# Two points per VectorE operation, and units of scores folded across eight steps

## The chip, the cores and the metric

The kernel runs on one core of one Trainium2 chip, everything in float32. The metric is device time in microseconds, the median of repeated executions of the whole program. PE is TensorE, DVE VectorE, ACT ScalarE, POOL GpSimd, SP SyncE.

## The reference, cut to what matters

Four layers run one after another on x of shape (2, 512, 32, 32). The change lies in the first, a deformable attention with 8 groups of 64 channels, whose keys are 64 sampled points per group. For each of 2 x 8 groups, 1024 pixels (queries) and 64 points (keys) a small network gives a bias from the pixel's position relative to the point:

```python
pos  = grid_q[:, :, None, :] - grid_kv[:, None, :, :]          # (16, 1024, 64, 2)
bias = sign(pos) * log1p(abs(pos))
bias = relu(bias @ cpb_w1 + cpb_b1)                            # 2 -> 128   first layer
bias = relu(bias @ cpb_w2 + cpb_b2)                            # 128 -> 128 second layer
bias = (bias @ cpb_w3 + cpb_b3).reshape(b, GROUPS, H*W, Hd*Wd) # 128 -> 1   third layer
sim  = einsum('bhid,bhjd->bhij', qh, kh) + bias
attn = softmax(sim, axis=-1)
out  = einsum('bhij,bhjd->bhid', attn, vh)
```

Then follow a projection, an MLP, and three more attention layers, which the change leaves alone.

## The kernel before

**Tiles, steps, points.** Layer 0 works through NT = 8 tiles of scores. A tile holds two groups: 128 points on the partitions and 1024 pixels along them. It is made in 32 steps of four points, so the main loop has 256 steps; t is the tile of a step i, i // 32.

**First layer (`first`, L599).** The sign-log of the position splits into a part in x and a part in y, each a table of 32 numbers per point. The tables of a tile are written to DRAM (`slog_d`, L471), read back for 16 points at a time, broadcast over the partitions (`load_tabs`, L573), and scaled by `cpb_w1`. One DVE operation per point adds the x row and the y row for 32 x 32 pixels and clamps at zero; its result, 128 hidden units by 1024 pixels, goes to one of the 11 places of `ring`. It is issued 7 points ahead of its use (AHEAD).

**Second layer (`second`, L616, L625).** The 128 hidden units of the second layer are sorted by the sign of `cpb_w3` into four parts of 32. For each part PE multiplies four points side by side (128x32 weights, each point in its own 32 columns of the array) for two halves of 512 pixels into `z`; ACT adds the bias and takes the relu. The four points of a step are on partitions 32 point to 32 point + 31.

**Joins and folds.** DVE joins parts 0 and 1 and parts 2 and 3 with the turned sign (`joined`, L630). The rest of the sum over hidden units is done by DMA: the second join is added to the first (L934, issued from GpSimd), then the partitions of a unit are folded in half (L927), and in half again, now into the shared unit of four steps: for the unit's first step in place (L929), for the three others by a copy on SP (L931) of one half and an add on GpSimd (L937) of the other. `joins[i]` is the unit of step i; its room comes from six places of `bridge` for units that others are folded into, and from a ring of four (`h2j`) for the others.

**Third layer (`third`, L645).** Four shared units (16 steps) at a time are multiplied by weights of plus and minus ones (`w3_16`), which sum what is left over partitions and put each point in its row of `sim`. That is done twice per tile, at steps 20 and 36 counted from the tile's first. Then `scores` (L653) adds query times key, and `finish` does the softmax in the steps behind (ACT copy, PE transposes, DVE maximum, ACT exponentials).

The order in each engine is that of the program (`in_order`): each of the four parts of a step (k = 0 to 3) issues its own pieces. The generator `behind` puts the softmax of the last tile (`finish`), the offsets of the tile after next (`offsets`, with DVE reductions at L414) and the samples of the next (`samples`) into the same order, one piece after every second part. The last 16 steps use units of two steps, and the loop ends in `finish_last`.

A buffer comes free when its last reader is done; the framework's waits are semaphores between engines and on DMAs. GpSimd's and SP's queues are in order too: a DMA whose wait isn't met holds those behind it.

Of the kernel before, what the change touches and what calls it, by code (L numbers as in the profile page):

```python
# [12 lines left out]
F32 = mybir.dt.float32  # L13
# [6 lines left out]
P = 128  # L20
# [59 lines left out]
def kernel(ctx: ExitStack, tc: tile.TileContext, a: dict, out: bass.AP):  # L80
# [111 lines left out]
    def layer0(l0, fold_d, t2_b, o2_b):  # L192
# [6 lines left out]
        h2q = l0.enter_context(tc.tile_pool(name="att_h2q", bufs=3))  # L199
        h2p = cycle([bridge[:, k, :] for k in range(6)])  # L200
        h2j = cycle([bridge[:, 6, :], bridge[:, 7, :], *(one.tile([P, HW], F32, name=f"h2j{k}") for k in range(2))])
# [18 lines left out]
        qkw = next(h2j).rearrange("p (j q n) -> p j q n", j=2, q=NPAIR)  # L220
# [15 lines left out]
        ring = [one.tile([P, HW], F32, name=f"h1{k}") for k in range(3)]  # L236
        ring += [qkv2.rearrange("p k n -> p (k n)")[:, k * HW : (k + 1) * HW] for k in range(6)]
        ring += [proj2.rearrange("p k n -> p (k n)")[:, k * HW : (k + 1) * HW] for k in range(2)]
# [13 lines left out]
        ones = one.tile([P, P], F32, name="ones")  # L252
        nc.gpsimd.memset(ones, 1.0)
# [25 lines left out]
        w3_16 = one.tile([P, 48], F32, name="w3_16")  # L279
# [7 lines left out]
        def bias_weights():  # L287
            sort = h2b.tile([P, 7, P], F32, name="sort", tag="h2")
            row, below, w2t = [sort[:, k, :] for k in range(3)]
            perm = sort[:, 3:, :].rearrange("p b (r u) -> p b r u", u=32)  # L290
            few = one.tile([P, 28], F32, name="few")
# [69 lines left out]
            quarter = few[:, 26:28]  # L361
            for k in range(2):
                nc.vector.tensor_reduce(quarter[:, k : k + 1], ident[:, 2 + k : P : 4], AX.X, ALU.add)
                nc.vector.scalar_tensor_tensor(eighth, quarter[:, k : k + 1], 8.0, eighth, ALU.mult, ALU.add)
            nc.vector.tensor_scalar(w3_16[:, 16:32], row[:, 0:16], eighth, 0.0, ALU.add, ALU.is_equal)
            nc.vector.tensor_scalar(w3_16[:, 16:32], w3_16[:, 16:32], w3sign[:, 1:2], None, ALU.mult)
# [15 lines left out]
        def offsets(t):  # L382
# [88 lines left out]
            nc.sync.dma_start(out=slog_d[t].rearrange("x p i -> p x i"), in_=pos)  # L471
# [13 lines left out]
        def samples(t):  # L485
# [25 lines left out]
            wx = one.tile([P, P], F32, name="wx")  # L511
# [17 lines left out]
            shift = one.tile([P, P], F32, name="shift")  # L529
# [12 lines left out]
            kq = one.tile([P, P], F32, name="kq")  # L542
# [3 lines left out]
            values = one.tile([P, P], F32, name="values")  # L546
# [12 lines left out]
        NCH = NR // 4  # L559
        LAST = NT * NR - 16  # L560
        tabs_of = {}

        def load_tabs(c):
# [4 lines left out]
            for ax in range(2):  # L568
                src = slog_d[t, ax].rearrange("(q r) i -> q r i", q=4)
                tab = two.tile([P, 16, 32], F32, name=f"tab{ax}")  # L570
                if 4 * c < LAST:
                    q, r = rc % 4, rc // 4 * 16
# [16 lines left out]
        def first(p):  # L589

            chunk, point = divmod(p, 16)
            if point == 0:
                tabs_of.pop(chunk - 1, None)
                if chunk + 1 < NT * NCH:
                    load_tabs(chunk + 1)
            tx, ty = tabs_of[chunk]
            h1 = ring[p % len(ring)]

            nc.vector._custom_dve(  # L599
                TENSOR_ADD_SAT,  # L600
                out=h1.rearrange("p (y x) -> p y x", x=W),
                in0=tx[:, point, :].unsqueeze(1).to_broadcast([P, H, W]),
                in1=ty[:, point, :].unsqueeze(2).to_broadcast([P, H, W]),
                s0=float(np.finfo(np.float32).max),
                s1=0.0,
            )
            return h1

        def second(i, h1s, part):
# [3 lines left out]
            for half in range(2):  # L613
                n = slice(half * HALF, (half + 1) * HALF)
                for point in range(4):
# [3 lines left out]
                        h1s[point][:, n],  # L619
# [3 lines left out]
            ring = h2q if part % 2 else h2b if part else h2j if i % (4 if i < LAST else 2) else h2p  # L623
            h2 = ring.tile([P, HW], F32, name="h2", tag="h2") if ring in (h2q, h2b) else next(ring)
# [10 lines left out]
        def third(sim, r, h2s, fours=(), halves=range(2), wide=False):  # L635

            for half in halves:
                n = slice(half * HALF, (half + 1) * HALF)
                w = w3_16[:, 16 - r : 48 - r] if wide else w3[:, 24 - r : 56 - r]
# [17 lines left out]
        def finish(t, sim):  # L657
# [4 lines left out]
            simb = one.tile([P, HW], F32, name="simb", tag="simb")  # L662
# [11 lines left out]
            at = one.tile([P, 8, P], F32, name="at", tag="simb")  # L674
# [42 lines left out]
        def finish_last(sim, eights, fours, right_sums, left_sums):  # L717
# [7 lines left out]
            simb = one.tile([P, HW], F32, name="simb", tag="simb")  # L725
# [90 lines left out]
        nat = [[next(h2p).rearrange("p (k n) -> p k n", k=2) for _ in range(2)] for _ in range(3)]  # L816
# [68 lines left out]
        h1s, parts, joins, sim, w1s = {}, {}, {}, None, None  # L885
        behind = chain(small_steps, offsets(1), samples(0))
        AHEAD = 7

        for p in range(AHEAD):
            h1s[p] = first(p)  # L890
        late_loads()
        for i in range(steps):
            for k, part in enumerate((1, 0, 3, 2)):
# [3 lines left out]
                if p < 4 * steps:  # L897
                    h1s[p] = first(p)
                due = i - 20
                if k == 1 and 0 <= due < LAST and due % 16 == 0:  # L900
                    t, r = divmod(due, NR)
                    if r == 0:
                        sim = ps_s.tile([P, HW], F32, name="sim")
                    third(sim, r, [joins.pop(due + j) for j in range(0, 16, 4)], wide=True)
                    if r:
# [10 lines left out]
                if LAST <= i - 2 and i < steps - 2:  # L916
# [4 lines left out]
                    if i - 3 >= LAST and i % 2 and k == 3:  # L921
                        nc.gpsimd.dma_start(out=joins[i - 3][1:P:2], in_=joins.pop(i - 2)[1:P:2], accum_op=ALU.add)
                if 0 <= i - 2 < LAST:
                    j = (i - 2) % 4
# [1347 lines left out]
```

## Time and profile before

| | |
|---|---|
| median of 3 runs | 3350.77 us (3349.29 to 3352.3) |
| the profiled execution | 3353.46 us, of which span 3351.7 us |
| granted PE clock, mean | 0.998 |
| main loop of layer 0 | from 59.6 us, its last step's joins at 1983.5 us |
| first layer, L599 | 1024 operations, mean 1216 ns |
| joins, L630 | 512 operations, mean 1276 to 1277 ns |
| second layer, L616 | 16384 matmuls, each about 593 ns, four at a time |
| third layer, L645 | 280 matmuls |

Times in a profile are from one execution, counted from the start of its span. L12 is line 12 of the kernel. In a line of a group or of the timeline, `out<-in` are the names of the tiles, xN is the number of instructions; "idle before" or a bracket is the time in which the engine stood still ahead of it, with what ended that. PEld is the loading of weights, which overlaps PE. A line of the table of stretches gives, for each of PE, PEld, DVE, ACT and POOL, the busy us (and the instructions), then the granted clock, the share in which the DMA engines were busy, and GB/s.

### The profile page before, as it was taken

To read this page: it belongs to the slowest core of one execution; us is meant where nothing else is said; L and a number is where in the kernel's file an instruction comes from. 1 tells how busy PE (TensorE), PEld (TensorE's weight loads), DVE (VectorE), ACT (ScalarE), POOL (GpSimd) and SP (SyncE) were. 2 spreads that over 40 slices of the span, in tenths; PEclk is the share of its full clock that TensorE was granted. 3 is DMA by queue.
4 is the path that set the end of the run, shared out by engine and by line. 5 is a ranking of instruction groups with operands and counts; after the bars stand their busy time and mean duration, and the time that the engine had idled before them with its cause. 6 is when DMAs were issued, how large, how long until landed. Compare 5 with 4: busy or idle time off the path is not lost.

```text
span 3351.7 us, 61808 instructions
## 1 busy us (share of the span) xinstructions
PE 3323.8 (99%) x24813; PEld 1611.7 (48%) x24813; DVE 2673.0 (80%) x3540; ACT 1805.5 (54%) x2774; POOL 676.7 (20%) x804
## 2 busy tenths in 40 slices
PE   9999999999999999999999999999999999999999
PEld 4333333332333332333333339999953443687777
DVE  6999999999999799999999976455446465665556
ACT  4866877877877577877877652122136245122221
POOL 0333333333333233333333310000000000000000
PEclk9999999999999999999999999999999999999999
DMA  5778787787787577787787751000100000000111
GB/s 166 157 161 166 153 168 156 152 166 153 158 167 155 103 162 155 159 169 152 158 166 157 161 135 58 14 8 14 52 0 14 26 29 20 7 7 3 30 32 36
DMA packets 142488, 343.97 MB, mean 103 GB/s; under 512 B 36464, under 2 KB 51440, under 8 KB 141424
## 3 DMA queue, kind: packets, MB, share of 16 engines
q0 software_dynamic: 68400, 231.26, 36.5%
q1 hardware_dynamic: 72496, 103.95, 10.7%
q8 instruction: 197, 3.23, 0.4%
q10 hardware_dynamic: 1296, 4.72, 0.4%
q14 instruction: 99, 0.81, 0.1%
HBM read 71.46 MB, written 10.83 MB: 25 GB/s over the span
## 4 chain that ended last, share of the span: by engine, by line
PE 82%; DVE 9%; issue 5%; DMA 2%; ACT 1%; POOL 1%; DVEq 0%; SPq 0%; POOLq 0%; ACTq 0%
PE z L616 38%; PE pma L135 6%; PE pw L1435 6%; PE pmb L135 5%; PE pmv L1435 4%; PE score L1614 3%; PE pv L1626 3%; DVE wa L599 3%; PE pm L1435 3%; PE score L1435 3%; PE pmt L1435 1%; PE ppr L1435 1%; DVE h L599 1%; DMA bridge<-h 1%; DVE bridge L630 1%
## 5 line engine op out<-in xcount | busy, mean ns | idle before, releaser
L616 PE MATMUL z<-wa,cpb_w 128*32 128x512 f32 x11904 | 1779.2, 593 | 5.8 <-ACT h L625 3.7
L625 ACT ACTIVATE h<-z,b2h 128x1024 f32<-128x1024 f32 x768 | 851.3, 1114 | 347.9 <-PE z L616 310.6
L616 PE MATMUL z<-h,cpb_w 128*32 128x512 f32 x4480 | 983.2, 593 | 1.6 <-ACT h L625 1.6
L616 PEld LDWEIGHTS z<-wa,cpb_w 128*32 128x32 f32 x11904 | 497.2, 110 | 888.2 <-issue 778.1
L599 DVE CUSTOM_DVE_ANT_1 wa<-tab,tab 128x1024 f32<-128x1024 f32 x744 | 878.1, 1216 | 1.3 <-PE z L616 1.1
L616 PEld LDWEIGHTS z<-h,cpb_w 128*32 128x32 f32 x4480 | 256.6, 110 | 328.6 <-issue 292.1
L599 DVE CUSTOM_DVE_ANT_1 h<-tab,tab 128x1024 f32<-128x1024 f32 x280 | 332.9, 1216 | 2.3 <-PE z L616 2.2
L630 DVE SCALAR_TENSOR_TENSOR h<-h,turn,h 128x1024 f32<-128x1024 f32 x256 | 326.8, 1276 | 4.3 <-ACT h L625 4.3
L625 ACT ACTIVATE bridge<-z,b2h 128x1024 f32<-128x1024 f32 x162 | 180.8, 1116 | 121.4 <-PE z L616 119.0
L927 POOL DMA_DIRECT2D bridge<-bridge x150 | 127.6, 850 | 547.2 <-DMA bridge<-h 510.5
L630 DVE SCALAR_TENSOR_TENSOR bridge<-bridge,turn,h 128x1024 f32<-128x1024 f32 x162 | 206.8, 1277 | 4.2 <-ACT bridge L625 4.2
L934 POOL DMA_DIRECT2D bridge<-h x161 | 163.4, 1015 | 213.2 <-DVE h L630 123.6
L1278 ACT COPY p<-pma 128x128 f32<-128x128 f32 x80 | 21.3, 266 | 334.7 <-PE pma L135 334.7
L1270 DVE TENSOR_TENSOR upper<-pma,p 128x256 f32<-128x256 f32 x80 | 33.7, 422 | 178.6 <-ACT p L1278 178.5
L1615 ACT ACTIVATE p<-score 128x512 f32<-128x512 f32 x256 | 130.0, 624 | 81.2 <-PE score L1614 79.6
L927 POOL DMA_DIRECT2D h2j<-h2j x90 | 76.2, 847 | 323.0 <-DMA h2j<-h 293.6
L1647 DVE TENSOR_TENSOR acc<-acc,p 128x1024 f32<-128x1024 f32 x96 | 111.0, 1217 | 19.4 <-ACT p L1615 19.3
L625 ACT ACTIVATE h2j<-z,b2h 128x1024 f32<-128x1024 f32 x94 | 105.0, 1117 | 37.9 <-PE z L616 37.3
L1614 PE MATMUL score<-q,k 64*128 64x512 f32 x512 | 120.7, 604 | 1.1 <-DVE gm L1191 1.1
L630 DVE SCALAR_TENSOR_TENSOR h2j<-h2j,turn,h 128x1024 f32<-128x1024 f32 x94 | 120.0, 1276 | 0.0
L1626 PE MATMUL pv<-p,vT 128*64 128x512 f32 x512 | 116.5, 598 | 0.0
L937 POOL DMA_DIRECT2D bridge<-h2j x90 | 111.9, 1244 | 2.6 <-issue 1.8
(458 smaller groups left out, 4379.8 us busy)
## 6 DMA issues: line engine op xcount, KB each, us to landing
bridge<-h POOLq DMA_DIRECT2D x161, 512.0 KB, 5.5
h2j<-h POOLq DMA_DIRECT2D x94, 512.0 KB, 5.9
bridge<-bridge POOLq DMA_DIRECT2D x159, 256.0 KB, 3.9
tab<-slog_d SPq DMA_DIRECT2D x128, 256.0 KB, 4.6
h2j<-h2j POOLq DMA_DIRECT2D x90, 256.0 KB, 3.2
bridge<-bridge POOLq DMA_DIRECT2D x150, 128.0 KB, 5.4
bridge<-bridge SPq DMA_DIRECT2D x90, 128.0 KB, 3.7
bridge<-h2j SPq DMA_DIRECT2D x90, 128.0 KB, 3.6
```

The costliest lines, as they stand in the source:

```text
L135: nc.tensor.matmul(pm, w, m, start=(k == 0), stop=(k == len(pairs) - 1))
L599: nc.vector._custom_dve(TENSOR_ADD_SAT, out=h1.rearrange("p (y x) -> p y x", x=W), in0=tx[:, point, :].unsqueeze(1).to_broadcast([P, H, W] ...
L616: nc.tensor.matmul(z[point * 32 : point * 32 + 32, n], cpb_w2[:, lo : lo + 32], h1s[point][:, n], start=True, stop=True,)
L625: nc.scalar.activation(h2, z, AF.Relu, bias=b2h[:, part : part + 1])
L630: nc.vector.scalar_tensor_tensor(h2, h2, turn[:, part // 2 : part // 2 + 1], parts.pop(part + 1), ALU.mult, ALU.add)
L927: nc.gpsimd.dma_start(out=own[0:P:2], in_=own[1:P:2], accum_op=ALU.add)
L934: nc.gpsimd.dma_start(out=joins[i - 1], in_=other, accum_op=ALU.add)
L937: nc.gpsimd.dma_start(out=joins[i - 3 - j][j:P:4], in_=joins.pop(i - 3)[2:P:4], accum_op=ALU.add)
L1435: nc.tensor.matmul(out, stationary(l, k), moving(r, k), start=start and k == 0, stop=k == nk - 1, skip_group_check=not start,)
L1614: nc.tensor.matmul(sc, ks[m][r, s * P : (s + 1) * P], qs[m][r, n], start=True, stop=True)
L1615: nc.scalar.activation(p[:, part], sc, AF.Exp, scale=64 ** -0.5)
L1626: nc.tensor.matmul(pv[half][part * 64 : part * 64 + 64], vt[s % 4][:, lo : lo + 64], lps[s, half][:, part, :], start=(s == 0), stop=(s == 7),)
```

## The change

1. One DVE operation of `first` makes two points. The y table is stored in DRAM with the two points of a pair interleaved, by two DMAs of single numbers beside the one for x. The results of a pair lie interleaved by rows of 32 pixels, so `second` reads each point as 16 runs of 32. `ring` has 6 places of two points, AHEAD is 8.
2. For the first seven tiles a shared unit holds eight steps instead of four: every unit is folded in half twice and then a third time into the shared unit, one step later. The third layer then runs once per tile, at step 37 counted from its first, with the weights `w3_32`. In the last tile the units are as before.
3. Room for units comes from one queue of ten places (`room`), to which a place returns when its unit has been folded away or read by the third layer. ACT's results of parts 1 and 3 get four places in place of three (`h2q`). A few small tiles share places to make room.
4. `bias_weights` makes the further weights, with more small DVE operations; its `ones` is set by DVE.

```diff
-        h2q = l0.enter_context(tc.tile_pool(name="att_h2q", bufs=3))
-        h2p = cycle([bridge[:, k, :] for k in range(6)])
-        h2j = cycle([bridge[:, 6, :], bridge[:, 7, :], *(one.tile([P, HW], F32, name=f"h2j{k}") for k in range(2))])
+        h2q = l0.enter_context(tc.tile_pool(name="att_h2q", bufs=4))
+        room = deque([bridge[:, 7, :], *(one.tile([P, HW], F32, name=f"h2j{k}") for k in range(2))])
+        room += [bridge[:, k, :] for k in range(7)]
...
-        ring = [one.tile([P, HW], F32, name=f"h1{k}") for k in range(3)]
-        ring += [qkv2.rearrange("p k n -> p (k n)")[:, k * HW : (k + 1) * HW] for k in range(6)]
-        ring += [proj2.rearrange("p k n -> p (k n)")[:, k * HW : (k + 1) * HW] for k in range(2)]
+        ring = [one.tile([P, 2 * HW], F32, name=f"h1{k}") for k in range(2)]
+        ring += [qkv2.rearrange("p k n -> p (k n)")[:, k * 2 * HW : (k + 1) * 2 * HW] for k in range(3)]
+        ring.append(proj2.rearrange("p k n -> p (k n)"))
...
+            digit = few[:, 26:29]
+            for k, (lo, step) in enumerate(((2, 4), (3, 4), (4, 8))):
+                nc.vector.tensor_reduce(digit[:, k : k + 1], ident[:, lo:P:step], AX.X, ALU.add)
...
+            for lo in range(5, 8):
+                nc.vector.tensor_reduce(odd, ident[:, lo:P:8], AX.X, ALU.add)
+                nc.vector.tensor_add(digit[:, 2:3], digit[:, 2:3], odd)
+            nc.vector.scalar_tensor_tensor(eighth, digit[:, 2:3], 16.0, eighth, ALU.mult, ALU.add)
+            nc.vector.tensor_scalar(w3_32, row[:, 0:32], eighth, 0.0, ALU.add, ALU.is_equal)
...
-            nc.sync.dma_start(out=slog_d[t].rearrange("x p i -> p x i"), in_=pos)
+            nc.sync.dma_start(out=slog_d[t, 0], in_=pos[:, 0, :])
+            pairs = slog_d[t, 1].rearrange("(a k) i -> a (k i)", k=2).rearrange("a (i k) -> k a i", k=2)
+            with nc.allow_non_contiguous_dma("4096 numbers"):
+                for k in range(2):
+                    nc.sync.dma_start(out=pairs[k], in_=pos[k:P:2, 1, :])
...
+        WIDE = (NT - 1) * NR
         LAST = NT * NR - 16
+
+        def shared(i):
+            return 8 if i < WIDE else 4 if i < LAST else 2
...
-            tx, ty = tabs_of[chunk]
-            h1 = ring[p % len(ring)]
+            tx, ty = [tab[:, point : point + 2, :] for tab in tabs_of[chunk]]
+            h1 = ring[p // 2 % len(ring)].rearrange("p (y k x) -> p y k x", k=2, x=W)
             nc.vector._custom_dve(
                 TENSOR_ADD_SAT,
-                out=h1.rearrange("p (y x) -> p y x", x=W),
-                in0=tx[:, point, :].unsqueeze(1).to_broadcast([P, H, W]),
-                in1=ty[:, point, :].unsqueeze(2).to_broadcast([P, H, W]),
+                out=h1,
+                in0=tx.unsqueeze(1).to_broadcast([P, H, 2, W]),
+                in1=ty.rearrange("p k y -> p (k y)")
+                .rearrange("p (y k) -> p y k", k=2)
+                .unsqueeze(3)
+                .to_broadcast([P, H, 2, W]),
...
-            return h1
+            return [h1[:, :, k, :] for k in range(2)]
...
-                        h1s[point][:, n],
+                        h1s[point][:, half * 16 : half * 16 + 16, :],
...
-        AHEAD = 7
+        AHEAD = 8
...
-                if p < 4 * steps:
-                    h1s[p] = first(p)
-                due = i - 20
-                if k == 1 and 0 <= due < LAST and due % 16 == 0:
-                    t, r = divmod(due, NR)
-                    if r == 0:
-                        sim = ps_s.tile([P, HW], F32, name="sim")
-                    third(sim, r, [joins.pop(due + j) for j in range(0, 16, 4)], wide=True)
-                    if r:
+                if p < 4 * steps and k % 2 == 0:
+                    h1s[p], h1s[p + 1] = first(p)
+                for due, n in ((i - 37, 8), (i - 20, 4)):
+                    if k != 1 or not 0 <= due < LAST or due % NR or shared(due) != n:
+                        continue
+                    t = due // NR
+                    sim = ps_s.tile([P, HW], F32, name="sim")
+                    third(sim, 0, [taken(due + j) for j in range(0, 4 * n, n)], wide=w3_32 if n == 8 else w3_16)
+                    if n == 8:
                         assert next(behind, None) is None
                         scores(t, sim)
...
-                    j = (i - 2) % 4
-                    whole, own = joins[i - 2 - j], joins[i - 2]
+                    own, n = joins[i - 2], shared(i - 2)
+                    whole, j = joins[i - 2 - (i - 2) % n], (i - 2) % n
                     if k == 0:
                         nc.gpsimd.dma_start(out=own[0:P:2], in_=own[1:P:2], accum_op=ALU.add)
-                    if k == 3 and j == 0:
+                    if k == 3 and (n == 8 or j == 0):
                         nc.gpsimd.dma_start(out=own[0:P:4], in_=own[2:P:4], accum_op=ALU.add)
-                    if k == 3 and j:
+                    elif k == 3:
                         nc.sync.dma_start(out=whole[j:P:4], in_=own[0:P:4])
+                if k == 2 and 0 <= i - 3 < WIDE:
+                    own, j = joins[i - 3], (i - 3) % 8
+                    if j:
+                        nc.sync.dma_start(out=joins[i - 3 - j][j:P:8], in_=own[0:P:8])
+                    else:
+                        nc.gpsimd.dma_start(out=own[0:P:8], in_=own[4:P:8], accum_op=ALU.add)
...
-                j = (i - 3) % 4
-                if k == 1 and 0 <= i - 3 < LAST and j:
-                    nc.gpsimd.dma_start(
-                        out=joins[i - 3 - j][j:P:4], in_=joins.pop(i - 3)[2:P:4], accum_op=ALU.add
-                    )
+                for at in (i - 4, i - 3):
+                    if k != 1 or at < 0 or at >= LAST or (shared(at) == 8) != (at == i - 4):
+                        continue
+                    n = shared(at)
+                    j = at % n
+                    if j:
+                        own = taken(at)
+                        nc.gpsimd.dma_start(
+                            out=joins[at - j][j:P:n], in_=own[n // 2 : P : n], accum_op=ALU.add
+                        )
```

`taken(i)` takes the unit of step i out of `joins` and returns its place to `room`.

## The prediction

> **What bounds the kernel now.** I read the page first, for the shares and the chain that ended last.
>
> ```profile
> span 3351.7 us, 61808 instructions
> PE 3323.8 (99%) x24813; PEld 1611.7 (48%) x24813; DVE 2673.0 (80%) x3540; ACT 1805.5 (54%) x2774; POOL 676.7 (20%) x804
> ```
>
> Everything that the change touches lies in layer 0, whose loop over 256 steps runs from 59.6 to about 1982 us. So the next views are of that loop: busy time in one stretch of 238 us (one tile of scores, 32 steps), then the chain in order of time near the loop's end.
>
> ```profile
> 300.00:538.00 238.00, 236.94 (x2152) 75.10 (x2148) 232.53 (x213) 180.55 (x251) 83.84 (x97) 1.00 0.78 159
> ```
>
> ```profile
> 1899.82 49.78 PE z L616 x464
> 1949.61 1.72 PE sim L645 x16
> 1951.32 30.90 PE z L616 x288
> ```
>
> PE is busy for 236.94 of 238 us and DVE for 232.53: two engines near their limit. The chain is PE. Its 464 records are 116 passes of four matmuls side by side, 49.78 / 116 = 0.429 us a pass; 16 passes make a step, 6.87 us. The third layer (L645) stands in that chain as 1.72 us, four passes, with nothing beside it on PE.
>
> DVE's timeline, in a stretch without other work:
>
> ```profile
> 254.25 2.35 DVE L599 CUSTOM_DVE_ANT_1 wa<-tab,tab 128x1024 f32<-128x1024 f32 x2
> 256.53 1.28 DVE L630 SCALAR_TENSOR_TENSOR bridge<-bridge,turn,h 128x1024 f32<-128x1024 f32 x1
> 257.72 2.35 DVE L599 CUSTOM_DVE_ANT_1 wa<-tab,tab 128x1024 f32<-128x1024 f32 x2
> ```
>
> Two first-layer operations take 2.28 us start to start and a join 1.19, so DVE needs 2 x 3.47 = 6.94 us a step where PE needs 6.87. DVE loses 0.07 us a step there and about 0.9 in each step with a reduction of `products` (L414, mean 971 ns). The timeline shows where this leads: a join starts 1.9 us behind the ACT result that it reads in step 43 and 7.3 to 7.5 us behind in steps 49 to 51. Then PE pauses:
>
> ```profile
> 450.62 3.62 PE L616 MATMUL z<-wa,cpb_w 128*32 128x512 f32 x32
> 454.78 1.50 PE L616 MATMUL z<-wa,cpb_w 128*32 128x512 f32 x12 [0.55 <-ACT h L625]
> ```
>
> Eight passes from 450.62 should end at 454.05; the next starts 0.73 later. Adding up all starts of passes from 59.6 to 1992 us, pauses of over 0.12 us sum to 14.7 us: 1.9 are waits of L645 for a fold (1.46 and 0.39), 0.9 lies in the last tile's finish, and 11.9 come where DVE is late (mostly 0.7 behind `po` and 0.7 some steps later, in each tile). So PE's own work is the bound, and DVE's lateness is worth at most 12 us.
>
> Third comes GpSimd's queue, which issues the accumulating DMAs in order.
>
> ```profile
> 269.40 0.83 POOL L927 DMA_DIRECT2D bridge<-bridge  x1 [4.55 <-DMA bridge<-h]
> 269.93 1.22 POOL L934 DMA_DIRECT2D bridge<-h  x1
> 270.50 1.51 POOL L937 DMA_DIRECT2D bridge<-h2j  x1
> 275.68 0.86 POOL L927 DMA_DIRECT2D bridge<-bridge  x1 [3.67 <-DMA bridge<-h]
> ```
>
> The fold in half (L927) waits until the add of the same unit (L934) has landed, 5.5 us after its issue: a cycle of 6.28 us. Where a tab load comes between, it is 8.66 (281.99 to 290.65). Four cycles, 263.10 to 290.65, average 6.89 us a step. That is as much as PE's 6.87; the queue keeps up because a tile of 238 us holds 18 us beside PE's 32 x 6.87 = 220.
>
> **The change, part by part.** (1) Third layer. Before, 15 wide calls of 1.72 us (due 0, 16, ... 224); after, seven over a tile of 32 steps and one for the last tile: seven fewer. They lie on PE, the path: -12.0 us. Nothing in the trace could fill their place.
>
> (2) Two points in one DVE operation. The same elements, half the instructions. From plain two-input operations of 512 and 1024 numbers (L1717 692 ns, L1647 1217) a further 1024 cost 1.05 us, so a pair takes 1.14 + 1.05 = 2.19 start to start against 2.28, and a step 6.76 against 6.94: below PE's 6.87. Bounds: above, a reduction that reads with a stride costs 1.78 ns a number (L414: 971 ns for 448, 857 for 384), which would make a pair 3.65 us and DVE the bound at about 9.7 us a step; below, 2.19. I take 2.19, because the runs of 32 numbers and the zero steps are those of L599 now, which at 1216 ns costs what a plain operation costs (1217). What it is worth is not DVE's 0.18 us x 256 = 46 us but PE's pauses. With one more buffer for ACT's results (h2q, 3 to 4) too, I let 9 of the 11.9 us go: -9. What is late next is PE itself.
>
> [...]
>
> (3) The moving operand. A point's 512 columns are now 16 runs of 32, a gap of 32 between. 4096 passes depend on it, so 1% of pitch is 17.5 us. Bounds: the matmul with single numbers 512 bytes apart,
>
> ```profile
> L1752 PE MATMUL pb<-proj,vb x8: 1047/1090/1339, 2621.5 to 2622.7; 128*32 128x512 f32 x8
> ```
>
> has its second pass 0.9 us after the first, twice the 0.43; the permuted weights (L343, runs of 32, next run 128 on) take 356 and 275 ns for their two passes, as the contiguous L843. I take the latter, 0, being the same run length.
>
> (4) The fourth fold. GpSimd issues per step: 512, 256 and 128 KB (three steps of four as an add into the shared unit), after: 512, 256, 128 and 64. SP's copies fall from 128 KB in three of four steps to 64 in seven of eight. Bytes: 992 to 1016 KB a step, 2%. The new wait is the issue of the third fold, which stands on GpSimd until the second has landed (3.25 us after its issue in quiet cycles); queued behind it is the next unit's L927, which waits for its own landing at 6.3 anyway. Issue at 3.55 and 0.85 to 1.2 of work leave about 1.5 us. So the cycle stays 6.89, cost 0; the other end is 128 KB moved ahead of the next add, +0.65 us (192 KB/us while that queue runs), 7.5 a step. A unit's room is held a step longer, and the last fold of a tile is issued two steps (13.7 us) ahead of its third layer, as now. With PE quicker, the queue's lateness grows by 1 to 2 us; I take the waits of L645 from 1.9 to 5: +3.
>
> (5) The pair layout in DRAM: `slog_d` is written by three DMAs in place of one, two of them in single numbers.
>
> ```profile
> slog_d<-pos SPq DMA_DIRECT2D x8, 32.0 KB, 3.7
> vb<-in_vb SPq DMA_DIRECT2D x1, 6.0 KB, 5.2
> ```
>
> 1536 single numbers (`vb`) landed in 5.2 us, so 2 x 2048 take between 5 and 12 where 3.7 stood (1.6 for tile 0). For tile 0 the cover is 52.78 - 44.66 = 8.1 us between the scaled tab and the first point, which waits for PE's `pb`; without it 3 to 9 us would show. For the six later tiles no tab waits, but SP's copies queue behind, and GpSimd's adds behind those; the room there has two to four buffers spare. I take +1 in all, 0 to +20.
>
> [...]
>
> (6) Setup: some eleven more DVE operations of 0.15 to 0.23 us, 2 us, under the same 8.1 us; six pairs before the first join against eleven points, 13.1 against 12.5 us, while the first two pairs are ready at 57.2 and PE folds weights until 59.64: 0.
>
> Sum: 3353.5 (the profiled execution; span 3351.7) - 12 - 9 + 3 + 1 = 3336.5. The median of the runs, 3350.8, lies 2.7 below the profiled one: 3334.
>
> **The rivals.** (A) DVE's relief turns into nothing, as the pauses move to GpSimd's folds: only the third layer goes, and 3 to 8 us come back as waits of L645: 3342 to 3347. For it: four cycles of 6.89 against 6.87. Against: the two waits so far were 1.9 us in all.
>
> (B) Slower: GpSimd's chain becomes the bound. Place: L927's wait for L934's landing, with one more fold in the queue. A tile is then 31 cycles and one long step (that of the scores, 11.6 us in steps 132 and 196). PE will need 238 - 1.7 - 1.3 = 235 us a tile, so the chain binds from a cycle of (235 - 11.6) / 31 = 7.21 and makes the kernel slower than now from 7.30. At 7.4 a tile takes 241 us, +3 x 7 = +21 in all, at 6.89 + 0.65 = 7.54 it is +49: 3358 to 3400. For it: DMA engines 78% busy, 0.4 us of slack a step. Against: the new fold's data (0.65 us) fit the 1.4 us in which that queue stands still each cycle.
>
> (C) The paired layout doesn't save: PE reads the runs 2% slower (+35 - 12) or DVE's pair costs 2.5 us (then DVE needs 7.38 a step, and with the 10 us of its other work in a tile, 232.5 - 32 x 6.94, 246 us, +56): 3374 and beyond.
>
> **How the numbers follow.** Forecast 0.60 (own range 3326 to 3343), A 0.14, B 0.17, C 0.09. About 0.2% (6.7 us) is what a measurement of this kernel can tell from no change: same is 3344 to 3357.5. Faster: 0.60 and half of A, 0.67. Slower: 0.09 and most of B, 0.23. Same: 0.10. The range reaches from 3325 to B's middle, 3370; outside lie C, B's upper half and 2% below.
>
> **What would show it.** Right: L645 with 7 x 16 = 112 fewer matmuls; L599 as 512 operations of about 2.27 us; PE's pitch 0.429; joins at most 4 us behind ACT in steps 49 to 51; GpSimd's cycle at 6.9. Wrong: a pitch above 0.433; a pair above 2.45 us; idle PE released by DMA ahead of L645 for over 2 us a tile; waits of GpSimd after the `slog_d` stores that reach ACT's part 0.

## The result, and the profile after

The changed kernel takes 3498.7 us, median of 5 runs (3493.7 to 3509.6), against 3350.6 for the kernel before: 1.0448 times as long, interval 1.0434 to 1.0462. The forecast was 3334, in a range that ended at 3370. The profiled execution took 3496.85 us, of which span 3495.1. Of the executions behind the medians below, one is left out because it ran at a granted clock of 0.65 (e5_third_later, 4952.9 us).

The page first: the span with the busy shares, the counts of DMA packets, and the chain that ended last.

```profile
span 3495.1 us, 61223 instructions
PE 3357.5 (96%) x24701; PEld 1603.9 (46%) x24701; DVE 2645.9 (76%) x3039; ACT 1792.0 (51%) x2774; POOL 857.4 (25%) x1027
...
DMA packets 179860, 349.45 MB, mean 100 GB/s; under 512 B 72496, under 2 KB 87472, under 8 KB 178800
...
PE 51%; DMA 33%; issue 6%; DVE 5%; POOL 4%; ACT 1%; SPq 1%; ACTq 0%; DVEq 0%; POOLq 0%
```

The last two of these lines for the kernel before:

```profile
DMA packets 142488, 343.97 MB, mean 103 GB/s; under 512 B 36464, under 2 KB 51440, under 8 KB 141424
...
PE 82%; DVE 9%; issue 5%; DMA 2%; ACT 1%; POOL 1%; DVEq 0%; SPq 0%; POOLq 0%; ACTq 0%
```

PE was 99% busy and has fallen to 96%. A third of the chain is now DMA; before it was 2%. Packets under 512 bytes have doubled, by 36000: 32768 of them are the single numbers (eight tiles of 4096), nearly all the others further packets of 4 bytes.

One tile in the table of stretches (us, then busy us of PE, PEld, DVE, ACT and POOL, granted clock, DMA share, GB/s):

```profile
388.80:644.60 255.80, 239.55 (x2128) 72.82 (x2120) 228.95 (x149) 177.59 (x250) 108.67 (x130) 0.97 0.89 150
```

A tile takes 255.8 us where it took about 237.5. DVE needs less (228.95 us busy, from 232.5 in 238), GpSimd more (108.67 from 83.84).

What the second and third layer cost on PE, from the chain in order of time in the last tile:

```profile
2037.48 1.72 PE sim L666 x16
2039.19 49.78 PE z L637 x464
```

116 passes in 49.78 us, 0.429 us a pass, to the digit what it was: reading runs of 32 costs PE nothing. DVE's timeline with the pair operation (L617) and the joins (L651):

```profile
329.46 1.28 DVE L651 SCALAR_TENSOR_TENSOR h<-h,turn,h 128x1024 f32<-128x1024 f32 x1
330.66 2.29 DVE L617 CUSTOM_DVE_ANT_1 h<-tab,tab 128x2048 f32<-128x2048 f32 x1
332.86 1.28 DVE L651 SCALAR_TENSOR_TENSOR bridge<-bridge,turn,h 128x1024 f32<-128x1024 f32 x1
```

A pair takes 332.86 - 330.66 = 2.20 us start to start, a join 1.20: a DVE step of 2 x (2.20 + 1.20) = 6.80, where 6.76 had been worked out. So the costs taken in parts 1 to 3 of the sum held. The time is lost elsewhere. GpSimd's timeline around one tile's table store, whose two single-number DMAs SP issued at 485.89 and 487.14:

```profile
486.17 0.84 POOL L955 DMA_DIRECT2D bridge<-bridge  x1 [1.06 <-DMA bridge<-bridge]
489.49 0.85 POOL L953 DMA_DIRECT2D bridge<-bridge  x1 [2.49 <-DMA bridge<-h]
490.38 0.88 POOL L966 DMA_DIRECT2D bridge<-h  x1
490.94 1.12 POOL L974 DMA_DIRECT2D bridge<-bridge  x1
508.10 0.84 POOL L955 DMA_DIRECT2D bridge<-bridge  x1 [16.03 <-DMA bridge<-bridge]
515.44 0.85 POOL L953 DMA_DIRECT2D bridge<-bridge  x1 [6.50 <-DMA bridge<-h]
```

L953 folds in half, L955 folds in quarters, L966 adds the second join, L974 adds into the shared unit. The fold issued at 489.49 usually lands 3.3 us later; here L955 waits for it until 508.10. The add issued at 490.38 lands at 515. PE at the same place:

```profile
499.45 3.62 PE L637 MATMUL z<-wa,cpb_w 128*32 128x512 f32 x32
502.89 3.62 PE L637 MATMUL z<-h,cpb_w 128*32 128x512 f32 x32
516.40 3.64 PE L637 MATMUL z<-h,cpb_w 128*32 128x512 f32 x16 [9.90 <-ACT h L646]
```

ACT can't write its next result, because the late add still has to read the old one, so PE's `z` isn't emptied. Over the run, ACT's waits for that add are (us in total, times, longest):

```profile
ACT h L646 <- DMA bridge<-h: 82.2, 20, 14.6
```

In the kernel before, all of ACT's waits for a DMA in the loop sum to 3.8 us. And the first passes behind the pause run at half speed: 16 records in 3.64 us where 32 took 3.62. Three stretches, the first during the store, the other two behind it:

```profile
486.00:508.00 22.00, 20.50 (x192) 5.75 (x184) 22.00 (x15) 15.06 (x27) 3.38 (x4) 1.00 1.44 62
...
516.40:520.00 3.60, 3.60 (x16) 0.59 (x16) 3.46 (x2) 1.17 (x2) 0.80 (x1) 0.50 1.04 227
520.70:522.50 1.80, 1.80 (x16) 0.42 (x16) 0.81 (x1) 1.80 (x3) 1.22 (x2) 1.00 0.63 123
```

During the store the DMA engines' busy shares sum to more than full (1.44) and they move 62 GB/s, where a quiet stretch (540 to 555 us) has 155. Behind it the granted clock is 0.50.

Adding up, over the trace, by how much PE's starts in the loop of layer 0 come later than the nominal pitch, by step of the tile: some 195 us after, 49 before. About 79 us lie in the steps of the stores (8 before), 23 in the waits of the third layer for the last fold (1.8 before), 30 in the last step of a tile and its fourth (9 before), 7 at the loop's start (1 before), 24 are passes at half clock.

### The profile page after: what moved, and what is told of

It is laid out like the page before. It is cut to its first block, busy times and chain, and to the rows that moved or that the text cites. A ratio compares the mean times of both kernels' runs of the same rounds, so it can differ in the third digit from the quotient of the medians.

```text
span 3495.1 us, 61223 instructions
## 1 busy us (share of the span) xinstructions
PE 3357.5 (96%) x24701; PEld 1603.9 (46%) x24701; DVE 2645.9 (76%) x3039; ACT 1792.0 (51%) x2774; POOL 857.4 (25%) x1027
## 3 DMA queue, kind: packets, MB, share of 16 engines
q8 instruction: 196, 3.21, 0.4%
## 4 chain that ended last, share of the span: by engine, by line
PE 51%; DMA 33%; issue 6%; DVE 5%; POOL 4%; ACT 1%; SPq 1%; ACTq 0%; DVEq 0%; POOLq 0%
DMA bridge<-h 20%; PE z L637 12%; DMA h2j<-h 7%; PE pma L135 6%; PE pw L1472 6%; PE pmb L135 5%; DMA bridge<-bridge 4%; PE pmv L1472 4%; PE score L1651 3%; PE pv L1663 3%; PE pm L1472 3%; PE score L1472 3%; POOL bridge L953 2%; PE ppr L1472 1%; PE pmt L1472 1%
## 5 line engine op out<-in xcount | busy, mean ns | idle before, releaser
L637 PE MATMUL z<-wa,cpb_w 128*32 128x512 f32 x10880 | 1216.2, 600 | 71.9 <-ACT h L646 52.9
L617 DVE CUSTOM_DVE_ANT_1 wa<-tab,tab 128x2048 f32<-128x2048 f32 x340 | 776.2, 2284 | 10.0 <-PE z L637 9.7
L637 PEld LDWEIGHTS z<-wa,cpb_w 128*32 128x32 f32 x10880 | 345.7, 111 | 902.5 <-issue 702.5
L637 PE MATMUL z<-h,cpb_w 128*32 128x512 f32 x5504 | 615.7, 596 | 22.8 <-ACT h L646 12.2
L617 DVE CUSTOM_DVE_ANT_1 h<-tab,tab 128x2048 f32<-128x2048 f32 x172 | 392.7, 2284 | 1.6 <-PE z L637 1.4
L637 PEld LDWEIGHTS z<-h,cpb_w 128*32 128x32 f32 x5504 | 173.7, 110 | 440.5 <-issue 353.9
L651 DVE SCALAR_TENSOR_TENSOR h<-h,turn,h 128x1024 f32<-128x1024 f32 x256 | 327.1, 1278 | 39.6 <-ACT h L646 39.5
L953 POOL DMA_DIRECT2D bridge<-bridge x184 | 157.1, 854 | 507.5 <-DMA bridge<-h 494.1
L651 DVE SCALAR_TENSOR_TENSOR bridge<-bridge,turn,h 128x1024 f32<-128x1024 f32 x197 | 251.8, 1278 | 25.4 <-ACT bridge L646 24.9
L966 POOL DMA_DIRECT2D bridge<-h x196 | 213.0, 1087 | 160.1 <-DVE h L651 152.7
L955 POOL DMA_DIRECT2D bridge<-bridge x174 | 153.3, 881 | 237.8 <-DMA bridge<-bridge 220.8
L974 POOL DMA_DIRECT2D bridge<-bridge x141 | 181.9, 1290 | 29.0 <-DMA bridge<-bridge 26.5
L605 ACT ACTIVATE tab<-tab,pc 128x512 f32<-128x512 f32 x126 | 96.5, 766 | 15.8 <-DMA tab<-slog_d 15.8
```

The lines of the kernel that those rows point to most:

```text
L617: nc.vector._custom_dve(TENSOR_ADD_SAT, out=h1, in0=tx.unsqueeze(1).to_broadcast([P, H, 2, W]), in1=ty.rearrange("p k y -> p (k y)") .rear ...
L637: nc.tensor.matmul(z[point * 32 : point * 32 + 32, n], cpb_w2[:, lo : lo + 32], h1s[point][:, half * 16 : half * 16 + 16, :], start=True, ...
L651: nc.vector.scalar_tensor_tensor(h2, h2, turn[:, part // 2 : part // 2 + 1], parts.pop(part + 1), ALU.mult, ALU.add)
L953: nc.gpsimd.dma_start(out=own[0:P:2], in_=own[1:P:2], accum_op=ALU.add)
L955: nc.gpsimd.dma_start(out=own[0:P:4], in_=own[2:P:4], accum_op=ALU.add)
L966: nc.gpsimd.dma_start(out=joins[i - 1], in_=other, accum_op=ALU.add)
```

## The experiments

Two theories were put up: the single-number stores cause nearly all of it (theory 1), or the fourth fold makes GpSimd's queue too slow whatever the stores do (theory 2).

**e1_rows: the changed kernel without single numbers.** The y table is interleaved on the chip.

```diff
...
-                    nc.sync.dma_start(out=pairs[k], in_=pos[k:P:2, 1, :])
...
+                nc.sync.dma_start(out=sgn[0 : P // 2, k, :], in_=pos[k:P:2, 1, :])
...
+            nc.vector.tensor_copy(both.rearrange("a i k -> a k i"), sgn[0 : P // 2])
...
+            nc.sync.dma_start(out=slog_d[t, 1].rearrange("(a k) i -> a (k i)", k=2), in_=both...)
```

> The changed kernel with one part altered: the y table of a tile is interleaved on the chip (two transfers of 64 rows of 128 bytes within SBUF, one small DVE copy) and stored in DRAM in rows of 256 bytes, so that no single numbers are moved. In the changed kernel PE's pauses beyond its nominal pitch sum to 195.7 us, against 49.4 in the kernel before: about 79 of it in the steps of the stores (phases 24 to 27 of a tile, and two places in the first tile), 24 as passes at half clock behind long pauses, 32 as the wait of the third layer for the last fold, 30 in the last steps of a tile and its phase 3. Theory 1, the single-number stores are the cause of nearly all of it, since the lateness of GpSimd's queue (lag of the second join's add, 21 us behind the stores, 8 to 14 at the tile's end) comes from them: 3335 to 3355 us, lag at a tile's end under 6 us, L645's counterpart waits under 1.5 us a tile. Theory 2, the fourth fold makes GpSimd's cycle 7.2 us where PE's step is 6.85, and this lateness builds up without the stores: only the stores' own pauses and most of the half clock go, 3385 to 3415 us, and the third layer still waits 3 us or more a tile.

Measured: 3374.5 us, 1.008 of before (1.0066 to 1.0094). 124 us of the 148 go with the stores, but 24 more than before remain: between the theories. The pauses of the store steps are gone; the third layer still waits 11.5 us for folds in the first seven tiles (the 14.9 in the expectation of e5_third_later is the whole excess of those steps). GpSimd's timeline in a quiet stretch:

```profile
544.61 0.85 POOL L958 DMA_DIRECT2D bridge<-bridge  x1 [2.28 <-DMA bridge<-h]
545.15 1.22 POOL L971 DMA_DIRECT2D bridge<-h  x1
547.03 0.78 POOL L979 DMA_DIRECT2D bridge<-bridge  x1 [0.66 <-issue]
548.84 0.84 POOL L960 DMA_DIRECT2D bridge<-bridge  x1 [1.04 <-DMA bridge<-bridge]
551.52 0.85 POOL L958 DMA_DIRECT2D bridge<-bridge  x1 [1.84 <-DMA bridge<-h]
...
559.51 0.85 POOL L958 DMA_DIRECT2D bridge<-bridge  x1 [3.35 <-DMA bridge<-h]
```

The cycle of the fold (now L958) is 6.91 us where it was 6.28; the next, with a table load, is 7.99. Some cycles are set by the queue alone: the second join is ready when the turn of its add comes. Over all of these ("queue-bound" below), the mean is 7.43 us, against 6.92 in the kernel before. PE's step in the quiet part of a tile is 6.87.

**e2_before_stores: the stores alone, on the kernel before.**

```diff
             nc.sync.dma_start(out=slog_d[t].rearrange("x p i -> p x i"), in_=pos)
...
+                for k in range(2):
+                    nc.sync.dma_start(out=pairs[k], in_=pos[k:P:2, 1, :])
```

`pairs` is here a view of a spare table that nobody reads.

> The kernel before, with the two single-number stores of each tile's y table added beside its own store, into a table that nobody reads. Theory 1 (the stores hold the DMA engines and SP's queue for about 20 us each time, and all else follows): PE pauses of 5 to 12 us beside each store, with passes at half clock behind them, +8 to +16 us a tile, 3420 to 3480 us. Theory 2 (the fold chain is the cause, and the stores only find it late): the chain of three folds has a cycle of 6.9 and one or two buffers to spare, so most of a store's 20 us is taken up by the room: 3351 to 3385 us.

Measured: 3430.5 us, +80 (1.024, 1.0224 to 1.0256). The stores slow the kernel by themselves, without the fold and the pair operation, and the buffers don't take them up. A tile goes from 237.5 to about 248 us.

**e3_fold_alone: the fold without the pair operation.** `first` issues two operations per pair; the table stays in rows. The room, the lead of 8 points and the four places for ACT's results are those of the changed kernel.

> The changed kernel without its first part: one DVE operation per point again, tables stored as in the kernel before, the points of a pair in two contiguous halves of a place of the ring. Units still fold over eight steps and the third layer runs once a tile. Theory 1: the fourth fold costs next to nothing, and 12 us of third layer go: 3338 to 3352 us. Theory 2: the chain's cycle of 7.2 us against DVE's 6.94 builds up lateness over the 20 quiet steps of each tile, the third layer waits 2 to 5 us a tile, and the kernel is at 3360 to 3390 us.

Measured: 3389.9 us, 1.0122 (1.0107 to 1.0138). Theory 2 for this part: with the fold the kernel takes 40 us more than the kernel before, so the fold costs that much more than it saves. Queue-bound cycles average 7.51 us, and the third layer waits 20 us in seven tiles.

**e4_pair_alone: the pair operation without the fold,** tables in rows.

```diff
-            return 8 if i < WIDE else 4 if i < LAST else 2
+            return 4 if i < LAST else 2
...
+                    third(sim, r, [taken(due + j) for j in range(0, 16, 4)], wide=w3_16[:, 16 - r : 48 - r])
```

> The changed kernel without its second part: two points in one DVE operation, tables interleaved on the chip and stored in rows as in the first experiment, but units of four steps and the third layer twice a tile, as in the kernel before. Both theories expect PE's pitch to stay 0.429 us and DVE's lateness to go: 3338 to 3348 us. If it is slower than the kernel before by more than 6 us, reading rows of 32 numbers or the pair operation costs something that neither theory has.

Measured: 3341.9 us, 0.9976 (0.9966 to 0.9986): faster than the kernel before by 8.2 us, and the chain that ended last is PE nearly throughout:

```profile
PE 96%; DVE 1%; DMA 1%; ACT 1%; issue 0%; SPq 0%; POOL 0%; DVEq 0%; POOLq 0%; ACTq 0%
```

A tile takes 235.6 us. So the first part of the change is worth about what was worked out for it (8.2 us, 9 taken), once its tables go another way.

**e5_third_later: the third layer one step later,** on e1_rows.

```diff
-                for due, n in ((i - 37, 8), (i - 20, 4)):
+                for due, n in ((i - 38, 8), (i - 20, 4)):
```

> The first experiment's kernel (rows of 256 bytes, pair operation, fold over eight steps) with the third layer one step later, 38 steps behind its tile's first in place of 37. There the third layer waited 14.9 us in the loop for the last fold, against 4.6 in the kernel with the pair operation alone, and 6.7 us went to passes at half clock behind longer pauses. Theory A, the fourth fold harms only by landing late for the third layer: the wait and most of the half clock go, 3356 to 3364 us. Theory B, GpSimd's queue is itself too slow in the quiet stretches (7.1 to 7.2 us a cycle against PE's 6.83): the lateness goes one step on, and PE then waits in ACT's place for room, or in the third layer as before: 3367 to 3380 us.

Measured: 3385.1 us, 11 more than e1_rows: beyond theory B's range, on its side. The third layer itself waits for no fold any more until the last tile, but PE's pauses in that step are larger (32 us of excess in the loop) and have another cause. ACT's waits (total, times, longest):

```profile
ACT bridge L651 <- DMA bridge<-bridge: 21.7, 14, 8.1
ACT bridge L651 <- DMA h2j<-bridge: 16.3, 4, 10.6
...
ACT h2j L651 <- DMA bridge<-h2j: 15.6, 3, 9.6
```

These are places for units whose last fold has not landed, since the third layer now gives its four back a step later.

**e6_dummy_add: one more DMA a step, that nothing waits for,** on e4_pair_alone.

```diff
...
                     nc.gpsimd.dma_start(out=joins[i - 1], in_=other, accum_op=ALU.add)
+                    if 4 <= i < WIDE:
+                        nc.gpsimd.dma_start(out=spare[i % 2 : P : 8], in_=spare[4 + i % 2 : P : 8], accum_op=ALU.add)
```

> The kernel with the pair operation alone (units of four steps, third layer twice a tile) with one more accumulating DMA of 64 KB a step on GpSimd's queue, on rows that nobody else reads, so that no fold waits for it; the queue then has four DMAs a step as with the fourth fold, but no new wait for a landing. One of the ten places for units is used for its rows. Theory A, the data and the issue of one more DMA a step are what costs (0.33 to 0.6 us a step): GpSimd's cycle goes to 7.1 to 7.3 us, tiles from 235.6 to 238 or more, 3358 to 3385 us. Theory B, it is the new wait (the third fold stands on the queue until the second has landed): the cycle stays under 6.9 and the time at 3340 to 3348 us.

Measured: 3387.7 us, 1.0116 (1.0093 to 1.0139). Theory A: it is the load on the queue; the new wait isn't needed for it. The second join's add, from issue to landing, in e4_pair_alone, e6_dummy_add and e1_rows (the last number of each line):

```profile
bridge<-h POOLq DMA_DIRECT2D x192, 512.0 KB, 5.3
```

```profile
bridge<-h POOLq DMA_DIRECT2D x198, 512.0 KB, 6.0
```

```profile
bridge<-h POOLq DMA_DIRECT2D x196, 512.0 KB, 6.1
```

64 KB that have nothing to do with the unit make its add land 0.7 us later, as the fourth fold does. The mean queue-bound cycle goes from 6.89 to 7.36 us. The 46 us more than in e4_pair_alone are not all of this kind, though: the dummy's rows take one of the ten places for units, and ACT's waits for a place grow from about 2 to 12 us. The cycle and the landing are what shows the load.

**e7_half_stores: half as many single numbers,** on the changed kernel.

```diff
-            nc.sync.dma_start(out=slog_d[t, 0], in_=pos[:, 0, :])
+            nc.sync.dma_start(out=slog_d[t].rearrange("x p i -> p x i"), in_=pos)
...
-                for k in range(2):
-                    nc.sync.dma_start(out=pairs[k], in_=pos[k:P:2, 1, :])
+                nc.sync.dma_start(out=pairs[1], in_=pos[1:P:2, 1, :])
```

> The changed kernel with half of the single numbers: the tables are stored in rows first, then only the second point of each pair is written again as 2048 single numbers (so the first point's rows are left in the wrong order). All single-number stores together cost 124 us by the first experiment (3498.7 against 3374.5). Theory A, a store costs PE what its 20 us exceed the slack of the buffers by (some 8 us of lateness): half as many numbers hold the queues for about 10 us, and far more than half of the cost goes: 3380 to 3405 us. Theory B, cost in proportion to the numbers: 3430 to 3445 us.

Measured: 3432.2 us. Half of 124 above 3374.5 would be 3436.6: theory B, roughly in proportion. The buffers have no slack that would take up the first half.

**e8_pair_stores: the fourth corner,** e4_pair_alone with the changed kernel's stores.

> The pair operation with the changed kernel's own single-number stores, but units of four steps and the third layer twice a tile: the fourth corner beside pair alone (3341.9), pair and fold with rows (3374.5) and pair, fold and single numbers (3498.7). The single numbers cost 80 us on the kernel before and 124 with the fold. Theory A, what a store costs depends on how much GpSimd's queue has to spare behind it (queue-bound cycles of 6.9 us without the fourth fold, 7.43 with it, PE's step 6.85): 80 to 95 us here, 3422 to 3437 us, and the rest, 30 to 45 us, is the two together. Theory B, a store costs the same in any case: 3460 to 3470 us.

Measured: 3435.8 us, theory A. With the pair operation in all four:

| | units of four steps | units of eight steps |
|---|---|---|
| table stored in rows | 3341.9 | 3374.5 |
| in single numbers | 3435.8 | 3498.7 |

The stores cost 94 us without the fold and 124 with it; the fold costs 33 and 63. So of the 148 us: -8 the pair operation, +94 the stores, +33 the fold (its 12 us of third layer already counted), +30 the two together. The time is in theory A's range, but its reason, that the queue without the fold has more to spare behind a store, isn't borne out by the traces: at the end of a tile the second join's add is still 6 to 10 us late in e8_pair_stores, nearly as late as in the changed kernel (8 to 10). What differs is the lateness right behind a store, 14 to 20 us at most without the fold and 17 to 27 with it. Why the two add up to more than their sum stays open.

**e9_more_room: eleven places for units,** on e5_third_later.

```diff
-        h2q = l0.enter_context(tc.tile_pool(name="att_h2q", bufs=4))
-        room = deque([bridge[:, 7, :], *(one.tile([P, HW], F32, name=f"h2j{k}") for k in range(2))])
+        h2q = l0.enter_context(tc.tile_pool(name="att_h2q", bufs=3))
+        room = deque([bridge[:, 7, :], *(one.tile([P, HW], F32, name=f"h2j{k}") for k in range(3))])
```

> The kernel with the third layer one step later (rows, pair, fold over eight steps), with eleven places for units in place of ten, taken from ACT's results of parts 1 and 3 (three places in place of four). In it PE's waits at that step (31.6 us in the loop) were waits of ACT for a place whose last fold had not landed. Theory A, room is what lacks: those waits go, a tile comes near the 235.6 us of pair alone less 1.7 of third layer, 3332 to 3350 us. Theory B, GpSimd's queue is the bound: its cycles average 7.43 us wherever it is late, so a tile can't be shorter than 32 x 7.43 = 237.8 us, whatever the room: 3356 to 3378 us.

Measured: 3360.8 us, 1.0032 (1.0019 to 1.0044): theory B by the time. Its wording was too strict: the first tile took 229.4 us and one later tile 235.7, the others 238 to 245, so lateness seems to be carried from tile to tile; the six tiles without further work in them average 238.2, near the 237.8 of 32 cycles. Room was part of the matter all the same: the eleventh place took 24 us off. The waits for places went from ACT's units to ACT's results that the second join's add still has to read:

```profile
ACT h L651 <- DMA bridge<-h: 18.4, 7, 4.2
ACT h L651 <- DMA h2j<-h: 8.9, 4, 3.7
```

**e10_pair_three: three places for ACT's results,** on e4_pair_alone (the first edit of e9_more_room alone).

> The kernel with the pair operation alone, and three places for ACT's results of parts 1 and 3 as in the kernel before, in place of four. If the shorter DVE step alone ends PE's pauses (joins start 0 to 1.5 us behind ACT in the quiet steps), the fourth place does nothing: 3339 to 3345 us. If the fourth place carried part of the 8 us: 3346 to 3350 us.

Measured: 3342.4 us, 0.9978 (0.9969 to 0.9987). The fourth place does nothing. That the shorter DVE step carries the gain is the likeliest reading; the longer lead, the places of two points and the one queue for room, which came with it, were not tested apart.

**e11_fold_no_tabs and e12_pair_no_tabs: queue made free another way,** on e9_more_room and on e10_pair_three.

```diff
+            if c >= 2:
+                tabs_of[c] = kept[c % 2]
+                return
```

The same condition stands in `scale_tab`, so the scaling of these tables on ACT goes too.

> The kernel with eleven places and the third layer one step later (rows, pair, fold over eight steps; 3360.8 us), without the loads of tables from the third chunk of 16 points on, and without their scaling: later points use the tables of the first two chunks, so the bias values are not those of the reference. That takes 512 KB per four steps off the DMA engines. Theory A, GpSimd's queue is the bound: its queue-bound cycles average 7.38 us there (7.12 the median, the ones beside a table load 8 and more); without the loads they come to about 7.1, a tile needs 32 x 7.1 = 227 us of queue, less than PE's 234, so PE is the bound again and what the third layer saves comes out: 3326 to 3340 us. Theory B, the landing of the last folds or the room still sets the pace, whatever the queue has to spare: 3350 to 3362 us.

> The control for the run beside it: the kernel with the pair operation alone and three places for ACT's results (3342.4 us), also without the loads and the scaling of tables from the third chunk on (the bias values are not the reference's). PE is its bound (a tile of 235.6 us, 1 to 2 us of waits for a DMA in all), so taking the loads off changes nothing by either theory: 3337 to 3343 us. If it falls below 3334, the loads cost something in another way, and the other run must be read against this one.

Measured: 3334.1 us with the fold (0.9953, 0.9939 to 0.9966) and 3341.3 without it (0.9975, 0.9966 to 0.9984). Theory A, and the control doesn't move. Queue-bound cycles come to 7.02 us with the fold, most tiles to 234.0 to 235.1, and the fold (with eleven places and the later third layer) is worth 7 us. What lacks in the changed kernel is the throughput of GpSimd's queue beside the other DMAs: the later third layer didn't help, an eleventh place only in part, and with the table loads gone the fold pays.

Of the versions that compute the reference, e4_pair_alone and e10_pair_three are the fastest, 8 us ahead of the kernel before.

## Why the prediction was wrong

**Step 5, the stores of the pair layout: +1 taken, 0 to +20 allowed, 124 measured.** This is the step that failed most. The landing alone was well sized: in the first tile, before any fold runs, the 4096 numbers go out in some 8 us, within the 5 to 12 of the step. But that price came from `vb`, which is read in at 5.3 and 2030.5 us, before and behind the loop, while no accumulate of GpSimd runs, and the cover was looked for at SP's queue, at the tables and in two to four spare buffers. That was the wrong place. The stores run beside GpSimd's accumulates, and the busy shares of the 16 DMA engines then sum to 1.44 (486 to 508 us); the same prediction had those accumulates as a chain with 0.4 us of slack a step. Among the folds the same numbers take 13 to 20 us, and GpSimd's packets of 4 KB fall from 30 to 50 per us to about 8, so that a fold lands after 18 us in place of 3.3. The sum had to ask for when L927 and L934 land during the store, not when the store does. The range had the same error: it ended at 20 us. The runs show how many packets of 4 bytes these stores are, 32768, and how long 4096 of them take among the folds; why they hold up the accumulates for so long, no run here shows.

**Step 4, the fourth fold: 0 taken, +0.65 us a cycle as the far end; +0.5 measured.** A mis-sized term. The value 0 rested on the 1.4 us in which the queue was seen to stand still each cycle. But that gap is the time from the issue of the fold in half to its first packet: 269.40 to 270.8 us in the kernel before. With the fourth fold it is still there (544.61 to 546.0 in e1_rows), and the stretch of packets behind it grows from 4.6 to 5.8 us. e6_dummy_add shows the price without any dependence: 64 KB and one more DMA, 0.47 us a cycle. The nearest row was the far end that the text gave itself, 128 KB at the queue's rate.

**Rival B had the place and the price for that part.** It said that the chain binds from 7.21 us, makes the kernel slower from 7.30, and 3358 to 3400 at 7.4 to 7.54. Without the stores the cycle is 7.43 and the kernel takes 3374.5 (e1_rows), without the pair operation 7.51 and 3389.9 (e3_fold_alone). Its argument against, that the data fit the gap, decided for the wrong side. Its chance of 0.17 was too low for a slack of 0.4 us a step. The measured 3498.7 lies beyond rival B too: no rival had the stores. Two slips in the prediction's text change nothing: at a cycle of 7.54 rival B's own rule gives a tile of 245.3 us, +51 in all and not +49, and in step 5 seven tiles store their tables in the loop, not six.

**Rival A** is inside the result: the third layer waits 23 us in the changed kernel where 3 to 8 were allowed, because the second join's add is 8 to 10 us behind at the tile's end. **Rival C** is out: the pitch is 0.429, the pair 2.284 us.

**Steps 1, 2, 3 and 6 held.** The third layer has 112 matmuls fewer, and PE's nominal work in the loop is 12.0 us less between e12_pair_no_tabs and e11_fold_no_tabs; 7 of it reach the time. The pair operation brought 8.2 us where 9 were taken, and the fourth place had no part in it. One sign named for it did not come: joins in steps 49 to 51 were to start at most 4 us behind ACT, and in e4_pair_alone they start 4.9 to 6.1 us behind, where it was 6.6 to 7.5 before. So the gain came although DVE made up only some 1.5 us of its lateness; how much lateness PE bears was not worked out. In e1_rows, with the table in rows, the first pass starts at 59.7 us as before; in the changed kernel at 62.4; over all profiles here it lies between 56 and 63, so this says little.

The list of what would show it wrong had the right line, waits of GpSimd after the `slog_d` stores that reach ACT, but the sum held one microsecond for it. A second line of that list came as well: the third layer waits 2.3 to 3.9 us for a DMA in each of the first seven tiles.

## What to carry to other kernels

When a change adds a DMA, price it by what the DMAs already in flight will land late, on every queue, and follow that to the buffers they hold; its own landing may harm nobody. A queue that kept up with 0.4 us to spare per step had no room here for another 64 KB a step, though nothing waited for them: compare a queue's mean cycle, table loads and all, with the step of the engine that it feeds. And run the parts of a combined change apart: here the pair operation gained 8 us, and the fold and the new stores buried it.

## What the runs showed of the hardware

A pause of PE of over about 2.5 us was mostly followed by 3 to 6 passes at half clock (0.85 us in place of 0.43), so that it cost 1.3 to 2.5 us more than its length; in the changed kernel 58 passes, 24 us. Over the traces of all kernels here, slow passes followed 7 of 49 pauses of 1.2 to 2.45 us, 31 of 44 up to 4 us, and all 26 longer ones; in the changed kernel alone, from 55 to 2150 us, 1 of 5, 9 of 11 and all 8. The traces show no sharp limit between 2 and 4 us: in the changed kernel a pause of 2.87 us was followed by slow passes, pauses of 3.21 and 3.38 us were not.

Single numbers and accumulating DMAs hindered each other here by far more than their bytes: in the 22 us of one store of 16 KB, 62 GB/s were moved where the kernel with the table in rows moves 168 in the same stretch, some 2.3 MB less. The line of e1_rows:

```profile
486.00:508.00 22.00, 21.64 (x202) 7.84 (x198) 21.95 (x16) 14.15 (x15) 10.77 (x15) 1.00 0.88 168
```

The cost in PE's time grew with the numbers, about 7.5 us per 2048 in each of eight tiles (57.7 / 8 = 7.2 from e7_half_stores, 124.2 / 16 = 7.8 for all).
